# Softmax denominators of a second attention folded by accumulating DMAs within SBUF, and three smaller edits

## The chip, the cores and the metric

The kernel runs on one core of a Trainium2 chip. The metric is device time in microseconds (us), the median of several executions. In the profile PE is the matrix engine (PEld its weight loads), DVE the vector engine, ACT the scalar engine, POOL the GpSimd engine and SP the engine that here only issues DMAs. SBUF is the on-chip memory, of 128 partitions, and PSUM the memory that PE writes its results into.

## The reference, cut to what matters

The input `x` is 16 images of 256 channels by 1024 pixels, float32. Each image goes through a first attention over its pixels (4 heads of 64 channels), with a residual, and then through a second block: group norm, attention (8 heads of 32 channels), residual, group norm, a two-layer MLP with gelu, residual.

```python
x = _L0_conv_ref(x, w_proj, b_proj, w_out, b_out)      # attention, 4 heads of 64, + x
x = x + attention(group_norm(x, gn1_w, gn1_b), qkv_w, proj_w, proj_b, phys_bias)
h = group_norm(x, gn2_w, gn2_b)
h = einsum('oc,bchw->bohw', mlp_w1, h) + mlp_b1        # 256 -> 1024
h = gelu(h)
h = einsum('oc,bchw->bohw', mlp_w2, h) + mlp_b2        # 1024 -> 256
return x + h
# in attention(): softmax over m of (q k * scale + phys_bias), then times v
```

The change concerns the softmax of the second attention. Its denominator, the sum of exp(score) over the 1024 keys, is one number for each head and query.

## The kernel before, in words

**Tiling.** Channels lie on partitions, in CC = 2 chunks of 128. Queries go in NT = 2 blocks `t` of TB = 512, keys in SB = 8 blocks `kb` of 128. A score tile has 128 keys on its partitions and 512 queries along them, so the sum over the keys is a sum over partitions and over key blocks.

**One item of the second attention (`attention_b`, L508).** An item is a pair (t, c): 512 queries and the G = 4 heads of one channel chunk. There are four items per image, in the order (1,0), (0,0), (0,1), (1,1) (L513). Each item is cut into four units of two key blocks, so an image has 16 units. For each unit:

- `scores` (L518) makes s_b on PE (L532) and e_b = exp(s_b) on ACT (L547).
- `add` (L553) sums the e_b of all key blocks on DVE into es_b (L563). An item's es_b is two tiles of 128 x 1024, that is 128 x 512 for each of its four heads; tag "es" has four buffers.
- `weigh` (L579) multiplies e_b by v on PE (acc_b, L584) and adds it up in res_b (L597).

**Denominators.** A step after an item's last `weigh`, `normalise` (L601) sums es_b over the partitions: four matmuls on PE (L606), one for each head, with 32 columns of (scaled) ones, `eones`, as weights and 512 columns of es_b passing through. The result den_b in PSUM is 128 x 512: 32 equal rows for each head. `denominators` (L357) then copies it on ACT into rd_b (L358; tag "full", one buffer for all items), takes one row of 32 by a DMA of SP's queue to 128 x 16 (sp_b, L363), takes the reciprocal on DVE (L367), writes it by a DMA to DRAM (row_b, L368), and reads it back, broadcast, by four DMAs into the same rd_b (L373). POOL adds up the denominators and their inverses for a check at the end (L369, L370). At last `scale` (L629) multiplies res_b by rd_b on DVE (L631). After the second chunk of a block t, `project` multiplies the block by the output weights on PE (the tiles j, L344).

**Steps.** `attention_a` and `attention_b` are generators; each `yield` ends a step. `run` (L1036) calls `later.tick()` after every step, which runs what was put off by `later.after(n, ...)`, and then the pieces of `fill` for that step: projections and MLP products of neighbouring images, for PE to do beside the second attention. With L625 the steps of an item's denominators are put off by (1, 1) and for an image's last item by (3, 5). The last item's `project` is `handed` (L635) to the next image's `attention_a`, which calls it at its unit n = SB + 4 (L486).

**Order of the instructions.** A planner in the build rearranges the emitted instructions on each engine by modelled times, within the dependences; instructions in `keep_in_program_order` keep theirs. So the order on an engine is near the emitted one and not the same.

**Between two images.** After `attention_b` of image b comes `attention_0` of image b + 1, in which the last item's denominators are finished beside the first units of `attention_a`. On SP's queue there lie in the same stretch the load of the MLP weights for image b (`load_blocks(1, ...)`, L1103, L278; 1.8 MB from DRAM), an output store (L1023, 256 KB) and the load of a later image's x (`load_x`, L1100, L322; 1 MB).

**Other places that the change touches.** `attention_a` (L384) has es_a tiles (L430) of the same tag "es". `v` in the projections of q, k and v copies PSUM to SBUF on ACT (L800). `mlp` has a hidden stage with gelu on ACT (L919, L931), after which the next exp of `attention_b` needs another table of ACT (15 `ACT_TABLE_LOAD` at L547). Of POOL's DMAs before, the profile has those at the start (L152 to L161), which load and store weights.

Of the kernel before, what the change touches and what calls it, by code (L numbers as in the profile page):

```python
# [11 lines left out]
ALU = mybir.AluOpType  # L12
# [42 lines left out]
def kernel(  # L55
# [144 lines left out]

    ebias = const.tile([P, HEADS1], F32, name="ebias")
    eones = const.tile([P, HEADS1, D1], F32, name="eones")

    def exp_bias():
        nc.scalar.activation(ebias, pb, AF.Exp)
        nc.vector.tensor_copy(eones, ebias.unsqueeze(2).to_broadcast([P, HEADS1, D1]))


    def scale_v():
# [9 lines left out]
    with ExitStack() as first:  # L219
        first_pass(  # L220
            first, tc, x, out,
            dict(
                wp=wp, bqk=bqk, pb=pb, bo=bo, g1w=g1w, g1b=g1b, g2w=g2w,
                g2b=g2b, pjb=pjb, m1b=m1b, m2b=m2b, wo=wo, wq=wq, wpj=wpj,
                m2b2=m2b2, gavg=gavg, mhalf=mhalf, ones=ones, eones=eones,
                bvo=bvo, at_start=at_start, load_rest=load_rest, exp_bias=exp_bias,
                scale_v=scale_v,
                make_blocks=make_blocks,
                in_range=in_range,
            ),  # L230
        )
# [15 lines left out]
def first_pass(ctx, tc, x, out, k):  # L247
# [106 lines left out]

    def denominators(key, den, d, full, waits, then):  # L357
        nc.scalar.copy(d, den)  # L358
        n = full.shape[1]
        w = 4 * TB // P  # L360
        spread = work.tile([P, w], F32, tag="spread", name=f"sp_{key}", bufs=2)
        row = dram.tile([4 * TB // n, n], F32, tag="row", name=f"row_{key}", bufs=4)
        nc.sync.dma_start(spread, d[::32].rearrange("p (a b) -> p a b", b=w))  # L363

        def invert():
            inverse = work.tile([P, w], F32, tag="inverse", name=f"inv_{key}", bufs=2)
            tc.keep_in_program_order(nc.vector.reciprocal(inverse, spread))  # L367
            nc.sync.dma_start(row.rearrange("r (a b) -> (r a) b", b=w), inverse)  # L368
            nc.gpsimd.tensor_add(dsum, dsum, spread)  # L369
            nc.gpsimd.tensor_add(isum, isum, inverse)  # L370
            num = P * n // (4 * TB)
            for r in range(P // num):
                nc.sync.dma_start(  # L373
                    full[r * num : (r + 1) * num], row[r].partition_broadcast(num)
                )
            later.after(waits[1], lambda: then(full))

        later.after(waits[0], invert)
# [5 lines left out]
    def attention_a(b, qT, kT, v, project):  # L384
# [4 lines left out]
        accs, held, sums = {}, {}, {}  # L389

        def scores(i, kb):
            t, c = items[i]
# [16 lines left out]
        def weigh(i, kb, e):  # L409
            t, c = items[i]  # L410
            if kb == 0:
                if i % 2:
                    acc = wide(f"acc_{key}_{i}", 2)
                    accs[i] = [acc[:, h, :] for h in range(2)]
                else:
                    accs[i] = [bank(f"acc_{key}_{i}_{h}", h) for h in range(2)]
            for h in range(2):
                for g in range(2):
                    nc.tensor.matmul(  # L419
                        accs[i][h][g * D : (g + 1) * D, :],  # L420
                        v[h * HALF : (h + 1) * HALF, kb, c * 2 + g],
                        e[h * HALF : (h + 1) * HALF, g, :],
                        start=(kb == 0),
                        stop=(kb == SB - 1),
                    )
            if kb == 0:
                held[i] = e
                return
            if kb == 1:
                sums[i] = work.tile([P, 2, TB], F32, tag="es", name=f"es_{key}_{i}", bufs=4)  # L430
            nc.vector.tensor_add(sums[i], held[i] if kb == 1 else sums[i], e)  # L431
            if kb == SB - 1:
                r = res[:, c, t * TB : (t + 1) * TB]
                one, two = accs.pop(i)
                nc.scalar.copy(r, one)
                nc.vector.tensor_add(r, r, two)
                if i == len(items) - 1:
# [70 lines left out]
    def attention_b(b, qT, kT, v, project):  # L508
# [1 line left out]
        G = P // D  # L510


        items = [(NT - 1, 0)]  # L513
        items += [(t, 0) for t in range(NT - 1)] + [(t, 1) for t in range(NT)]
        units = [(i, kb) for i in range(len(items)) for kb in range(0, SB, 2)]
        res, sums = {}, {}

# [34 lines left out]

        def add(i, kb, es, which):  # L553
            if kb == 0 and 0 in which:
                sums[i] = [
                    work.tile([P, 2, TB], F32, tag="es", name=f"es_{key}_{i}_{n}", bufs=4)
                    for n in range(G // 2)
                ]
            for n in which:
                if kb == 0 and n < G // 2:  # L560
                    continue
                d = sums[i][n % 2]
                ins = nc.vector.tensor_add(d, es[n % 2] if kb == 0 else d, es[n])  # L563
                if n:
                    tc.keep_in_program_order(ins)
# [1 line left out]


        def result(t):
            if t < NT - 1 and b == 0:  # L570
                return [
                    work.tile([P, TB], F32, tag="g", name=f"res_{key}_{t}_{c}", bufs=16)
                    for c in range(CC)
                ]
            tag = "res1" if t == NT - 1 else "res" if b < B - 1 else "q0"
            r = act.tile([P, CC, S if tag == "q0" else TB], F32, tag=tag, name=f"res_{key}_{t}")
            return [r[:, c, :TB] for c in range(CC)]

        def weigh(i, kb, es):  # L579
            t, c = items[i]  # L580
            acc = bank(f"acc_{key}_{i}_{kb}", 0)
            for m in range(2):
                for g in range(G):
                    nc.tensor.matmul(  # L584
                        acc[g * D : (g + 1) * D, :],
                        v[:, kb + m, c * G + g],
                        es[2 * m + g // 2][:, g % 2, :],
                        start=(m == 0),
                        stop=(m == 1),
                    )  # L590
            if t not in res:
                res[t] = result(t)
            r = res[t][c]
            if kb == 0:
                nc.scalar.copy(r, acc)
            else:
                nc.vector.tensor_add(r, r, acc)  # L597
            if kb == SB - 2:
                later.after(1, lambda: normalise(i, r, i == len(items) - 1))

        def normalise(i, r, last):  # L601
            t, c = items[i]
# [2 lines left out]
            for g in range(G):  # L605
                nc.tensor.matmul(  # L606
                    den[g * D : (g + 1) * D, :],
                    k["eones"][:, c * G + g],
                    sums[i][g // 2][:, g % 2, :],
                    start=True,  # L610
                    stop=True,
                )
            full = work.tile([P, TB], F32, tag="full", name=f"rd_{key}_{i}", bufs=1)
            if at_end:
# [6 lines left out]
                    nc.gpsimd.tensor_add(tot[:, :1], tot[:, :1], part)  # L621
                return
            denominators(
                f"{key}_{i}", den, full, full,
                (3, 5) if last else (1, 1),  # L625
                lambda full: scale(i, r, last, full),
            )

        def scale(i, r, last, full):  # L629
# [139 lines left out]
    def qkv(key, D, src, weights, b_qk, qT, kT, v_dst):  # L769
# [16 lines left out]
                )  # L786

        def v(n):
            ps = single(f"v_{key}_{n}")
# [10 lines left out]
            nc.scalar.copy(  # L800
                v_dst()[:, 2 * n : 2 * n + 2],
                ps.rearrange("p (b h d) -> p b h d", b=2, d=D),
            )
# [91 lines left out]
    def mlp(b, xb):  # L895
# [44 lines left out]
            gelu(0, 1, i, ps[:, 1, :])  # L940

        def finish(i):
            ps = open_sums.pop(i)
            products_of(i, [(7, ps[:, 0, :], False), (6, ps[:, 1, :], False)])
            rest = gs[1, 1, i]
# [3 lines left out]
            gelu(1, 1, i, rest)  # L949
            combine((1, 0), (0, 0), False, i)  # L950
            combine((0, 1), (1, 1), False, i)

        hidden = [
            lambda part=part, i=i: part(i)
# [138 lines left out]

    later.after(2, fold_bias)
    later.after(8, k["scale_v"])
    hidden, outputs = [], []
    last = NT * CC * SB // 2 - 1
    for b in range(B):
# [41 lines left out]
            now, end = outputs[:3], outputs[3:]  # L1140
        if not first:

            fill = {m: [piece] for m, piece in enumerate(own[:5:2] + own[1::2] + own[6:])}
            fill.update({len(own) + 3 * m: [piece] for m, piece in enumerate(now)})
            now = []

# [331 lines left out]
```

## Time and profile before

| | us |
|---|---|
| median of 3 runs | 3666.4 (3665.53 to 3667.68) |
| the profiled execution | 3666.7 |
| its span in the trace | 3664.9 |
| TensorE clock granted, mean | 0.999 |
| one image, from its unit to the same unit of the next | 226.4 |

The span is the time between the first and the last instruction; 1.8 us of the execution lie around it. The period of one image is the distance of the same instruction in two successive images late in the run (3228.21 and 3454.65). The core spends nearly the whole span in 16 such periods, and 15 passages from the second attention of one image to the first attention of the next.

The groups of most weight besides the ones shown in the prediction, in the page's form (line, engine, operation, out<-in, shapes, count, busy us, mean ns, idle before and who ended it):

```profile
L563 DVE TENSOR_TENSOR es_b<-es_b,e_b 128x1024 f32<-128x1024 f32 x768 | 899.3, 1219 | 243.8 <-ACT e_b L547 243.8
L547 ACT ACTIVATE e_b<-s_b 128x1024 f32<-128x1024 f32 (+1 forms) x1280 | 982.9, 864 | 132.2 <-PE s_b L532 132.0
L406 ACT ACTIVATE e_a<-s_a 128x1024 f32<-128x1024 f32 x512 | 521.2, 1025 | 360.0 <-PE s_a L398 347.6
L532 PE MATMUL s_b<-q,k 32*64 32x512 f32 x8192 | 519.7, 600 | 4.9 <-DVE res_b L597 1.6
L584 PE MATMUL acc_b<-e_b,v 128*32 128x512 f32 x4096 | 492.1, 598 | 0.0
```

PE's matmuls overlap: [...]the busy time divided by the count (519.7 / 8192 = 63 ns) is nearer to what one costs[...].

### The profile page before, as it was taken

How to read it: one execution, taken by the hardware profiler on the slowest of the kernel's cores; microseconds unless marked ns; L12 is line 12 of the kernel's file. 1: busy time of each engine (PE TensorE's matmuls, PEld its weight loads, DVE VectorE, ACT ScalarE, POOL GpSimd, SP SyncE). 2: the span in 40 equal slices, each digit the busy share in tenths (PEclk: the TensorE clock that was granted, in tenths of full speed). 3: DMA queues.
4: the chain of work that ended last, by engine and by line, in shares of the span. 5: the costliest groups of instructions: out<-in, count | busy, mean ns of one | idle time of the engine just before them, and what ended most of it. 6: DMA issues, size and time to landing. Idle time of an engine off the chain costs nothing.

```text
span 3664.9 us, 79373 instructions
## 1 busy us (share of the span) xinstructions
PE 3632.6 (99%) x34221; PEld 1346.2 (37%) x34221; DVE 2658.1 (73%) x3424; ACT 2154.3 (59%) x2832; POOL 129.5 (4%) x266
## 2 busy tenths in 40 slices
PE   9999999999999999999999999999999999999999
PEld 3433343333433334333343333434334343343433
DVE  4586777767777677776767777677777777767777
ACT  4665657556565655656556565564655656556572
POOL 3000000000000000000000000000000000000000
PEclk9999999999999999999999999999999999999999
DMA  4000110101101011010110101101011010100100
GB/s 147 10 17 29 55 33 14 51 30 54 33 14 51 30 54 33 14 51 31 53 33 20 51 27 51 33 19 50 27 51 33 19 50 29 50 33 31 47 28 27
DMA packets 66549, 138.36 MB, mean 38 GB/s; under 512 B 35630, under 2 KB 36398, under 8 KB 61966
## 3 DMA queue, kind: packets, MB, share of 16 engines
q1 hardware_dynamic: 63116, 126.64, 10.7%
q8 instruction: 270, 4.42, 0.5%
q0 software_dynamic: 1328, 6.17, 0.5%
q14 instruction: 89, 0.73, 0.1%
q10 hardware_dynamic: 1746, 0.40, 0.1%
HBM read 111.17 MB, written 21.23 MB: 36 GB/s over the span
## 4 chain that ended last, share of the span: by engine, by line
PE 91%; DVE 4%; ACT 3%; DMA 1%; issue 1%; SPq 0%; ACTq 0%; POOL 0%; DVEq 0%
PE s_a L398 12%; PE acc_b L584 12%; PE s_b L532 12%; PE acc_a L419 12%; PE m L344 10%; PE m L906 9%; PE qk_a L344 6%; PE qk_b L344 5%; PE v_a L344 3%; PE j L344 3%; PE v_b L344 2%; ACT e_b L547 2%; PE o L344 2%; PE den_b L606 1%; DVE g L962 1%
## 5 line engine op out<-in xcount | busy, mean ns | idle before, releaser
L563 DVE TENSOR_TENSOR es_b<-es_b,e_b 128x1024 f32<-128x1024 f32 x768 | 899.3, 1219 | 243.8 <-ACT e_b L547 243.8
L547 ACT ACTIVATE e_b<-s_b 128x1024 f32<-128x1024 f32 (+1 forms) x1280 | 982.9, 864 | 132.2 <-PE s_b L532 132.0
L406 ACT ACTIVATE e_a<-s_a 128x1024 f32<-128x1024 f32 x512 | 521.2, 1025 | 360.0 <-PE s_a L398 347.6
L398 PE MATMUL s_a<-q,k 64*64 64x512 f32 x4096 | 544.3, 593 | 0.0
L419 PE MATMUL acc_a<-e_a,v 64*64 64x512 f32 x4096 | 540.1, 589 | 0.0
L532 PE MATMUL s_b<-q,k 32*64 32x512 f32 x8192 | 519.7, 600 | 4.9 <-DVE res_b L597 1.6
L431 DVE TENSOR_TENSOR es_a<-es_a,e_a 128x1024 f32<-128x1024 f32 x384 | 473.9, 1234 | 64.8 <-ACT e_a L406 41.2
L584 PE MATMUL acc_b<-e_b,v 128*32 128x512 f32 x4096 | 492.1, 598 | 0.0
L344 PE MATMUL m<-g,w 128*32 128x512 f32 (+1 forms) x3320 | 404.3, 592 | 0.0
L532 PEld LDWEIGHTS s_b<-q,k 32*64 32x64 f32 x8192 | 170.9, 130 | 321.3 <-issue 130.9
L419 PEld LDWEIGHTS acc_a<-e_a,v 64*64 64x64 f32 x4096 | 187.9, 133 | 251.5 <-issue 218.4
L398 PEld LDWEIGHTS s_a<-q,k 64*64 64x64 f32 x4096 | 175.9, 133 | 246.7 <-issue 193.1
L563 DVE TENSOR_TENSOR es_b<-e_b,e_b 128x1024 f32<-128x1024 f32 x128 | 150.8, 1220 | 153.4 <-ACT e_b L547 153.4
L906 PE MATMUL m<-gn_h,w 128*128 128x512 f32 x512 | 243.7, 604 | 5.7 <-DVE g L932 3.3
L584 PEld LDWEIGHTS acc_b<-e_b,v 128*32 128x32 f32 x4096 | 108.5, 109 | 357.5 <-ACT e_b L547 194.7
L344 PE MATMUL qk_a<-x,wp 128*32 128x512 f32 (+1 forms) x1856 | 235.1, 593 | 4.1 <-ACT k L784 4.1
L344 PE MATMUL qk_b<-gn_g,wq 128*32 128x512 f32 (+1 forms) x1280 | 234.0, 592 | 0.0
L597 DVE TENSOR_TENSOR res_b<-res_b,acc_b 128x512 f32<-128x512 f32 x192 | 131.8, 686 | 129.8 <-PE acc_b L584 129.8
L344 PEld LDWEIGHTS m<-g,w 128*32 128x32 f32 (+1 forms) x3320 | 121.4, 112 | 262.3 <-issue 235.3
L962 DVE TENSOR_TENSOR g<-g,g 128x512 f32<-128x512 f32 x320 | 206.3, 681 | 4.0 <-ACT g L919 2.8
L906 PE MATMUL m<-hs,w 128*128 128x512 f32 x384 | 177.9, 592 | 0.1
L919 ACT ACTIVATE g<-g,m1b 128x512 f32<-128x512 f32 x128 | 92.2, 722 | 99.3 <-DVE g L946 72.2
(147 smaller groups left out, 2803.6 us busy)
## 6 DMA issues: line engine op xcount, KB each, us to landing
w<-w_kept SPq DMA_DIRECT2D x30, 1792.0 KB
d_a<-row_a SPq DMA_DIRECT2D x64, 256.0 KB
rd_b<-row_b SPq DMA_DIRECT2D x252, 64.0 KB
out_dram<-x SPq DMA_DIRECT2D x63, 256.0 KB
x<-in_x_dram SPq DMA_DIRECT2D x30, 512.0 KB
w_kept<-w_made POOLq DMA_DIRECT2D x2, 1792.0 KB, 6.0
w_made<-in_L_conv_mlp_w_dram POOLq DMA_DIRECT2D x8, 256.0 KB, 6.1
x<-in_x_dram SPq DMA_DIRECT2D x4, 256.0 KB
```

What stands on the lines that cost most here:

```text
L344: nc.tensor.matmul(o[sl], w[:, sl], r, **flags)
L398: nc.tensor.matmul(s[h : h + HALF, g, :], kT[g * D : (g + 1) * D, c, kb * P + h : kb * P + h + HALF], qT[g * D : (g + 1) * D, c, t * TB : ...
L406: nc.scalar.activation(e, s, AF.Exp, scale=float(D) ** -0.5)
L419: nc.tensor.matmul(accs[i][h][g * D : (g + 1) * D, :], v[h * HALF : (h + 1) * HALF, kb, c * 2 + g], e[h * HALF : (h + 1) * HALF, g, :], st ...
L431: nc.vector.tensor_add(sums[i], held[i] if kb == 1 else sums[i], e)
L532: nc.tensor.matmul(outs[g][h : h + HALF, :], kT[g * D : (g + 1) * D, c, k0 : k0 + HALF], qT[g * D : (g + 1) * D, c, t * TB : (t + 1) * TB] ...
L547: nc.scalar.activation(to, s, AF.Exp, scale=float(D) ** -0.5)
L563: ins = nc.vector.tensor_add(d, es[n % 2] if kb == 0 else d, es[n])
L584: nc.tensor.matmul(acc[g * D : (g + 1) * D, :], v[:, kb + m, c * G + g], es[2 * m + g // 2][:, g % 2, :], start=(m == 0), stop=(m == 1),)
L597: nc.vector.tensor_add(r, r, acc)
L906: nc.tensor.matmul(ps, blocks[1][number - 1][:, i * P : (i + 1) * P], inputs[b][number], start=first, stop=True, skip_group_check=not first,)
L962: (nc.vector.tensor_add if plus else nc.vector.tensor_sub)(d, d, gs[(*what, i)])
```

## The change

Four edits, cut to their core (line numbers in the diff are those of before, then after).

1. The items of every image go in the order of t: (0,0), (0,1), (1,0), (1,1). Which tags hold res_b changes with it, and so do the pieces of `fill` in the first and the last image.
2. For the first three items of an image, `fold` takes the place of the matmuls over es_b. es_b has four groups of 32 partitions, each holding, for all four heads, the sums over a quarter of the key positions (32 x 4 x 512 numbers, 256 KB). A DMA of SP's queue copies the first group, repacked, into a tile `packed` of 128 x 512, and the three other groups are added to it by three DMAs of POOL's queue with `accum_op=ALU.add`. Three steps later `normalise_folded` sums what is left with four matmuls of 128 columns each, with other weights (`folded`, made once at the start by a memset and eight small DMAs on POOL). den_b is then 128 x 128, and the ACT copy, the row and its broadcast (pieces of 512 bytes) have that shape. The fourth item keeps the old way, with (3, 5); the folded ones have (1, 1).
3. es_b of an item becomes one tile of 128 x 4 x 512 with two buffers, and es_a of two items one tile of the same tag.
4. Two ticks after the last `finish` of the hidden stage, `back_to_exp` runs an Exp on one column, and the first copy of v in the second attention's projection goes to DVE.

```diff
+    def fold_ones():
+        nc.gpsimd.memset(folded, 0.0)
+        g_num = P // D1
+        w = D1 // g_num
+        for c in range(HEADS1 // g_num):
+            for g in range(g_num):
+                nc.gpsimd.dma_start(
+                    folded[g::g_num, c, g * w : (g + 1) * w],
+                    eones[g::g_num, c * g_num + g, :w],
+                )
...
-        nc.sync.dma_start(spread, d[::32].rearrange("p (a b) -> p a b", b=w))
+        nc.sync.dma_start(
+            spread, d[:: 32 // parts].rearrange("p (a b) -> p a b", b=w)
+        )
...
-                sums[i] = work.tile([P, 2, TB], F32, tag="es", name=f"es_{key}_{i}", bufs=4)
+                if c == 0:
+                    both[t] = work.tile([P, 2 * CC, TB], F32, tag="es", name=f"es_{key}_{t}", bufs=2)
+                sums[i] = both[t][:, 2 * c : 2 * c + 2]
...
-        items = [(NT - 1, 0)]
-        items += [(t, 0) for t in range(NT - 1)] + [(t, 1) for t in range(NT)]
+        items = [(t, c) for t in range(NT) for c in range(CC)]
...
-                later.after(1, lambda: normalise(i, r, i == len(items) - 1))
+                if i == len(items) - 1:
+                    later.after(1, lambda: normalise(i, r, True))
+                else:
+                    fold(i, r)
+
+        def fold(i, r):
+            packed = work.tile([P, TB], F32, tag="packed", name=f"packed_{key}_{i}", bufs=1)
+            for j in range(G):
+                of = sums[i][j * D : (j + 1) * D]
+                if j == 0:
+                    nc.sync.dma_start(packed, of)
+                else:
+                    nc.gpsimd.dma_start(packed, of, accum_op=ALU.add)
+            later.after(3, lambda: normalise_folded(i, r, packed))
+
+        def normalise_folded(i, r, packed):
+            c = items[i][1]
+            q = TB // G
+            den = bank(f"den_{key}_{i}", 1)[:, :q]
+            for n in range(G):
+                nc.tensor.matmul(
+                    den[n * D : (n + 1) * D, :], k["folded"][:, c],
+                    packed[:, n * q : (n + 1) * q], start=True, stop=True,
+                )
+            full = work.tile([P, TB], F32, tag="full", name=f"rd_{key}_{i}", bufs=1)
+            denominators(
+                f"{key}_{i}", den, full[:, :q], full, (1, 1),
+                lambda full: scale(i, r, False, full), G,
+            )
...
         def finish(i):
+            if i == n4 - 1:
+                later.after(2, back_to_exp)
...
+        def back_to_exp():
+            one = small.tile([P, 1], F32, tag="part", name=f"one_{b}")
+            nc.scalar.activation(one, gs[1, 1, n4 - 1][:, :1], AF.Exp, scale=0.0)
...
+    later.after(9, k["fold_ones"])
...
-            fill = {m: [piece] for m, piece in enumerate(own[:5:2] + own[1::2] + own[6:])}
+            fill = {0: own[:1], 1: own[1:3], 2: own[4:5], 3: own[5:6], 4: own[3:4], 5: own[6:]}
```

More of the change, by code (lines that the diff above doesn't have):

```diff
@@ L202 @@
     eones = const.tile([P, HEADS1, D1], F32, name="eones")
+    folded = const.tile([P, HEADS1 * D1 // P, D1], F32, name="folded")
     def exp_bias():
@@ L226 @@
                 bvo=bvo, at_start=at_start, load_rest=load_rest, exp_bias=exp_bias,
-                scale_v=scale_v,
+                scale_v=scale_v, fold_ones=fold_ones, folded=folded,
                 make_blocks=make_blocks,
@@ L344, in product, with denominators @@
             nc.tensor.matmul(o[sl], w[:, sl], r, **flags)
-    def denominators(key, den, d, full, waits, then):
+    def denominators(key, den, d, full, waits, then, parts=1):
         nc.scalar.copy(d, den)
@@ L372, in invert @@
             for r in range(P // num):
-                nc.sync.dma_start(
-                    full[r * num : (r + 1) * num], row[r].partition_broadcast(num)
-                )
+                to, of = full[r * num : (r + 1) * num], row[r]
+                if parts > 1:
+                    to = to.rearrange("p (n q) -> p n q", n=parts)
+                    of = row.rearrange("r (a q) -> (r a) q", a=parts).rearrange(
+                        "(n g) q -> g n q", n=parts
+                    )[r]
+                nc.sync.dma_start(to, of.partition_broadcast(num))
             later.after(waits[1], lambda: then(full))
@@ L388, in attention_a @@
         res = act.tile([P, CC, S], F32, tag="res", name=f"res_{key}")
-        accs, held, sums = {}, {}, {}
+        accs, held, sums, both = {}, {}, {}, {}
         def scores(i, kb):
@@ L554, in add @@
             if kb == 0 and 0 in which:
[L555 to L558, printed above, removed]
+                sums[i] = work.tile([P, G, TB], F32, tag="es", name=f"es_{key}_{i}", bufs=2)
             for n in which:
@@ L561, in add @@
                     continue
-                d = sums[i][n % 2]
+                d = sums[i][:, n % 2 * 2 : n % 2 * 2 + 2]
                 ins = nc.vector.tensor_add(d, es[n % 2] if kb == 0 else d, es[n])
@@ L569, in result @@
         def result(t):
[L570 to L577, printed above, removed]
+            tag, n = ("hs", 3) if t == NT - 1 else ("res1", CC)
+            r = act.tile([P, n, TB], F32, tag=tag, name=f"res_{key}_{t}")
+            return [r[:, c] for c in range(CC)]
         def weigh(i, kb, es):
@@ L608, in normalise @@
                     k["eones"][:, c * G + g],
-                    sums[i][g // 2][:, g % 2, :],
+                    sums[i][:, g, :],
                     start=True,
@@ L623, in normalise @@
             denominators(
-                f"{key}_{i}", den, full, full,
-                (3, 5) if last else (1, 1),
-                lambda full: scale(i, r, last, full),
+                f"{key}_{i}", den, full, full, (3, 5), lambda full: scale(i, r, last, full)
             )
@@ L788, in v @@
         def v(n):
+            copy = nc.vector.tensor_copy if not n and b_qk is None else nc.scalar.copy
             ps = single(f"v_{key}_{n}")
@@ L799, in v @@
                     )
-            nc.scalar.copy(
+            copy(
                 v_dst()[:, 2 * n : 2 * n + 2],
```

## The prediction

> **What bounds the kernel now.** I read the page's busy times and the chain that ended last first, then the groups and waits of the operations that the change touches, then the timeline of one passage between two images.
>
> ```profile
> PE 3632.6 (99%) x34221; PEld 1346.2 (37%) x34221; DVE 2658.1 (73%) x3424; ACT 2154.3 (59%) x2832; POOL 129.5 (4%) x266
> PE 91%; DVE 4%; ACT 3%; DMA 1%; issue 1%; SPq 0%; ACTq 0%; POOL 0%; DVEq 0%
> ...
> L606 PE MATMUL den_b<-es_b,eones 128*32 128x512 f32 x512 | 67.4, 592 | 0.0
> L547 ACT ACT_TABLE_LOAD x15 | 19.2, 1283 | 0.3
> ...
> PE v_b L344 <- ACT e_b L547: 10.2, 15, 0.7
> ```
>
> PE sets the time: what is taken from PE is won, and where PE stands still it is lost. The denominators of the second attention are 67.4 us of busy time, and there is one wait of 0.7 us for an exp in each image but one. This is all there is to win. POOL is nearly empty.
>
> In the timeline (start, length, engine and line) the price of one item's denominator matmuls is the distance of neighbours:
>
> ```profile
> 1484.55 1.04 PE L584 MATMUL acc_b<-e_b,v 128*32 128x512 f32 x8
> 1485.41 1.04 PE L606 MATMUL den_b<-es_b,eones 128*32 128x512 f32 x8
> 1486.27 3.62 PE L344 MATMUL m<-g,w 128*32 128x512 f32 x32
> ```
>
> 0.86 us from den_b to the next work, for eight records (two for each float32 matmul), that is two rounds of 0.43 us over four column strips.
>
> The passage after an image's last item, where T = 1563.52 is the start of s_b of its last unit:
>
> ```profile
> 1563.52 1.97 PE L532 MATMUL s_b<-q,k 32*64 32x512 f32 x32
> 1567.16 3.62 PE L344 MATMUL j<-res_b,wpj 128*32 128x512 f32 x32
> 1570.60 3.62 PE L344 MATMUL m<-g,w 128*32 128x512 f32 x32
> 1568.02 3.49 DVE L563 TENSOR_TENSOR es_b<-es_b,e_b 128x1024 f32<-128x1024 f32 x3
> 1574.27 0.34 SPq L278 DMA_DIRECT2D w<-w_kept  x1
> 1577.47 1.04 PE L606 MATMUL den_b<-es_b,eones 128*32 128x512 f32 x8
> 1578.44 2.81 PE L398 MATMUL s_a<-q,k 64*64 64x512 f32 x24
> 1578.58 0.59 ACT L358 COPY rd_b<-den_b 128x512 f32<-128x512 f32 x1 [0.27 <-PE den_b L606]
> 1579.66 2.85 ACT L406 ACTIVATE e_a<-s_a 128x1024 f32<-128x1024 f32 x3 [0.49 <-PE s_a L398]
> 1583.66 0.38 SPq L368 DMA_DIRECT2D row_b<-inv_b  x1
> 1589.09 1.72 SPq L373 DMA_DIRECT2D rd_b<-row_b  x4
> 1592.72 0.69 DVE L631 TENSOR_TENSOR res_b<-res_b,rd_b 128x512 f32<-128x512 f32 x1 [3.98 <-DMA rd_b<-row_b]
> ```
>
> The reader is to see that PE goes from one group to the next, that ACT copies den_b at once into a free rd_b, and that transfers are slow here: the row, issued behind 1 MB of loads of x, lands after 5.4 us (1583.66 to 1589.09).
>
> [...]the trace of the start has 0.7 to issue and 2.2 to land (below), 2.9. [...]no trace here shows an accumulating DMA. [...]
>
> **The change part by part.**
>
> *Folded denominators, 48 of 64 items.* Four matmuls of 128 columns take the place of four of 512. Streaming falls from 0.43 to 0.107 us a round, and a round's weight loads (0.13 us for four at this shape) then set it: 2 x 0.13 = 0.26. Won: 0.60 each (0.55 to 0.64), x 48 = 28.6 us.
>
> *Their transfers.* One item: a copy by SP, then three accumulating DMAs on POOL, each waiting for the one before, as all write the same tile. The nearest rows:
>
> ```profile
> 32.93 3.02 POOL L152 DMA_DIRECT2D w_made<-in_L_conv_mlp_w_dram  x4 [6.00 <-DMA w_kept<-w_made]
> 38.19 2.07 POOL L160 TENSOR_TENSOR w_made<-w_made 128x512 f32<-128x512 f32 x1 [2.23 <-DMA w_made<-in_L_conv_mlp_w_dram]
> ```
>
> Issue 0.75 plus 2.23 is 3.0 us, and 0.8 for the second read (256 KB at the 323 GB/s that the queue moves when busy): 3.8. The first copy is 2.0 (the usual landing of sp_b) + 0.8 = 2.8. Chain: 2.8 + 3 x 3.8 = 14.1 us. It starts at the last add (T' + 8.0 in an item's last step, 1571.5) and PE wants it some two and a half steps of 7.2 us later, T' + 25: 17 us are there. So it is hidden up to 4.7 us for each accumulating DMA. [...] POOL's other work, the check sums, may be late at no cost.
>
> *Dummy Exp.* It moves the table load ahead of the first exp: 15 x 0.68 = 10.2 us won; at worst nothing.
>
> *Order of the items.* The number of matmuls is unchanged and so are the changes of tile shape. But the planner's order, read from the built program, is what counts. With t in order, item 2 is (1,0), and its denominators, due (1, 1), fall into the last step and the passage. The instructions of the passage, the same in 15 passages:
>
> ```
> SP   sp_b_2; w load (waits PE); row_b_2 (waits DVE); out store; rd_b_2 x4; x loads; sp_b_3
> DVE  adds of the last unit; reciprocal of item 2; x; res_b; es_a (2 adds); scale of item 2
> ACT  e_a 0 to 3; copy rd_b_3 <- den_b_3; e_a 4
> PE   den_b_3; s_a 0 to 2; acc_a half 0, kb 0; s_a 3; acc_a half 0, kb 1; s_a 4, one; acc_a half 1
> ```
>
> **A new wait.** rd_b has one buffer. The copy of item 3 must wait until item 2's scale has read it; before, that scale was done at T + 1.4, long ahead of the copy. Behind the waiting copy stand on ACT e_a 4 and all later exps; behind the copy on PE is acc_a half 1, since it takes the bank of den_b_3. Step by step: without j (3.44 us, now in another step) m ends at T + 7.1, so the w load is issued at T + 7.3 and s_a starts at S0 = T + 11.5 (14.9 less 3.44). The reciprocal is behind the adds (end T + 8.0), so the row is issued at T + 8.3, behind 1.8 MB. Load and store moved data until 6.9 us after the load's issue in this passage, so the row lands at T + 14.2. The broadcast ends 3.63 us after its first issue (1589.09 to 1592.72): T + 17.8. Scale 0.69, copy 0.6: acc_a half 1 starts at T + 19.3. From S0 that is 7.8 us, in which PE has 4.5 us of work: s_a 4 x 0.86, halves of acc_a 2 x 0.43, 0.2 of s_a 4. It loses 3.3, and 1.1 more since half 1 then runs alone on half of the array. 4.4 us a passage. From below: if the DMAs were free, scale still comes behind two es_a adds that need e_a 2 (S0 + 4.1): at the earliest scale ends at S0 + 6.0, which leaves 2.1 by standing still; with the adds one behind the other, 3.7 in all. From above 5.5, when x and store traffic delay the broadcast. 14 x 4.4 + 3.8 (the first, with a bare step) = 65.4. The last image has no passage, but its reciprocal goes into the same buffer: +3 (0 to 5).
>
> *Edits at nothing.* The eight small DMAs of `folded` lie at the start, and weights stored behind them are read 280 us later. The copies on ACT get shorter; ACT is at 59%. One copy of v to DVE: 0.6 us per image on an engine at 73%; DVE bounds bare steps alone (images 0 and 15). es_a and es_b have the same bytes and lifetimes. Scales of items 0 and 1 find their rows a step earlier than needed. Without this cover each is below 1 us an image.
>
> **Sum,** against the profiled execution, 3666.7: - 28.6 - 10.2 + 65.4 + 3.0 = 3696.3. The median is 0.3 below it, so 3696, 0.8% slower.
>
> **The rivals.**
>
> *A, as summed: the new wait costs more than the saving.* Per passage 3.4 to 5.5 us: 3677 to 3716. For it: the built order leaves no other way, and the only unmeasured part is how long. The saving is 38.8 us, so it decides from 38.8 / 15 = 2.6 us a passage.
>
> *B, the tile comes free early: faster.* Row and broadcast pass the weight load[...], and the half-filled array costs nothing because ACT had exps ready ahead. PE then stands still only from S0 + 4.5 to a copy at S0 + 6: 1.5 us. 3666.4 - 38.8 + 22.5 = 3650. Against it: the scale's place behind two adds on DVE.
>
> *C, accumulating DMAs late.* Above 4.7 us each, PE waits at the folded matmuls, three times the excess for some 45 items: at 5.2 another 67 us (3763), at 6.1 another 190 (3885). For it the landing of 6.1 on the page; against it the chain at the start, 3.0 for one.
>
> *D, they cancel.* 2.1 to 3.1 us a passage: within 7 us of 3666.
>
> **How the numbers follow.** A 0.57, B 0.20, C 0.13, D 0.10. 0.2%, 7.3 us, is about what a measurement of this kernel can tell. A and C are slower, 0.70; D the same, 0.10; B faster, 0.20. The predicted time is A's. The range takes in A, D and the nearer ends of B and C: 3648 to 3745, leaving out half of B and most of C; A's own is 3677 to 3716.
>
> **What would show it.** Right: den_b at half of its busy time or less, no table load between the gelu and v_b that PE waits for, and in each passage an idle time of PE and of ACT's copy of some 3 to 5 us, released by DVE's scale, which waits for rd_b. Wrong: the copy waits below 2 us (B or D), or PE waits for `packed` at the folded matmuls (C).

## The result, and the profile after

The changed kernel takes 3891.4 us (median of four, 3884.4 to 3896.0) against 3666.4 before: a ratio of 1.061, with a 95% interval from 1.059 to 1.063. It is slower by 225 us, where 30 were forecast.

The page of the changed kernel, its busy times and the chain that ended last:

```profile
PE 3720.7 (96%) x34221; PEld 1392.1 (36%) x34221; DVE 2670.0 (69%) x3440; ACT 2132.7 (55%) x2833; POOL 264.2 (7%) x419
PE 71%; DMA 19%; DVE 5%; issue 2%; SPq 1%; ACT 1%; ACTq 0%; DVEq 0%; POOLq 0%
```

DMA was 1% of the chain and is 19% now. PE does the same number of matmuls, 48 items of them shorter, and is busy 88 us longer: so the matmuls themselves ran slower. The mean granted clock is 0.978 instead of 0.999, and 2.1% of the span is 82 us. The waits of PE (engine, who waited for whom, us in total, times, longest):

```profile
PE den_b L631 <- DMA packed_b<-es_b: 81.1, 31, 6.7
PE acc_a L438 <- ACT rd_b L371: 46.6, 15, 4.6
```

The first is rival C, the second is forecast A. Both happened.

**The chain of accumulating DMAs.** The timeline of the first item of one image (start, length, engine and line; in brackets the idle time ahead and who ended it):

```profile
1572.23 0.60 SPq L621 DMA_DIRECT2D packed_b<-es_b  x1
1576.38 0.91 POOL L623 DMA_DIRECT2D packed_b<-es_b  x1 [44.38 <-PE m L357]
1581.33 0.90 POOL L623 DMA_DIRECT2D packed_b<-es_b  x1 [4.03 <-DMA packed_b<-es_b]
1586.43 0.88 POOL L623 DMA_DIRECT2D packed_b<-es_b  x1 [4.21 <-DMA packed_b<-es_b]
1591.34 0.42 PE L631 MATMUL den_b<-packed_b,folded 128*32 128x128 f32 x8 [1.73 <-DMA packed_b<-es_b]
```

From one accumulating DMA to the next are 5.1 us in the median: 0.9 to issue, 4.2 until the next can follow. The copy ahead takes 4.2 us. The chain takes 19.1 us here and 19 to 21 in every image. Of the 48 folded items 32 make PE wait: the first and second of every image, 1.6 to 3.5 us each in the middle images and up to 9 in the first and the last.

**The passage between two images.** Seven images in, the weight load, the row of the third item, its broadcast, scale, the copy and acc_a:

```profile
1670.38 0.35 SPq L291 DMA_DIRECT2D w<-w_kept  x1
1671.23 0.32 SPq L383 DMA_DIRECT2D row_b<-inv_b  x1
1678.68 1.74 SPq L394 DMA_DIRECT2D rd_b<-row_b  x4
1682.33 0.69 DVE L669 TENSOR_TENSOR res_b<-res_b,rd_b 128x512 f32<-128x512 f32 x1 [2.10 <-DMA rd_b<-row_b]
1683.10 0.59 ACT L371 COPY rd_b<-den_b 128x512 f32<-128x512 f32 x1 [2.94 <-DVE res_b L669]
1683.74 0.84 PE L438 MATMUL acc_a<-e_a,v 64*64 64x512 f32 x2 [2.97 <-ACT rd_b L371]
```

This is the forecast's chain, link by link: the row lands 7.4 us after its issue behind the load, the broadcast ends 3.65 us after its first issue, and PE stands still for 3.0 us. DVE had ended its two adds into es_a at 1680.23 and stood 2.1 us for the broadcast, so in the end the transfers set the time.

**The clock.** PE in two stretches of 3.41 us around that wait (stretch, us, busy, matmuls, granted clock, DMA share, GB/s):

```profile
1680.65:1684.06 3.41, 0.44 (x4) 1.00 0.85 235
1684.06:1687.47 3.41, 3.41 (x18) 0.50 0.35 120
```

After the wait the clock falls to half for 3.4 us, which costs 1.7 us more. This is what the busy time hides, and the forecast had left it out.

**Where the time is, by stage.** I call "passage" the distance from an image's first s_a to its first s_b, and "second attention" that from its first s_b to the next image's first s_a, both read from the trace. Passages before are 101.8 us long, after 110.1 in the median. The second attention of a middle image was 124.6 and is 128.3, that of the first image 90.2 and 112.6. Summed over the span: passages +124 us, second attention of the middle images +51, of the first image +22, and what follows the last image's first s_b +29. The two kinds of stage are the two axes of all experiments.

### The profile page after: what moved, and what is told of

It reads as the page before. It is cut to its first block, busy times and chain, and to the rows that moved or that the text cites. A ratio compares the mean times of both kernels' runs of the same rounds, so it can differ in the third digit from the quotient of the medians.

```text
span 3893.6 us, 79815 instructions
## 1 busy us (share of the span) xinstructions
PE 3720.7 (96%) x34221; PEld 1392.1 (36%) x34221; DVE 2670.0 (69%) x3440; ACT 2132.7 (55%) x2833; POOL 264.2 (7%) x419
## 4 chain that ended last, share of the span: by engine, by line
PE 71%; DMA 19%; DVE 5%; issue 2%; SPq 1%; ACT 1%; ACTq 0%; DVEq 0%; POOLq 0%
DMA packed_b<-es_b 13%; PE acc_a L438 12%; PE s_a L417 10%; PE s_b L552 9%; PE acc_b L596 7%; PE m L357 7%; PE m L945 6%; PE qk_b L357 5%; PE qk_a L357 3%; DMA row_b<-inv_b 3%; PE j L357 3%; PE v_b L357 3%; PE v_a L357 2%; PE o L357 2%; DMA rd_b<-row_b 1%
## 5 line engine op out<-in xcount | busy, mean ns | idle before, releaser
L438 PE MATMUL acc_a<-e_a,v 64*64 64x512 f32 x4096 | 626.0, 609 | 46.6 <-ACT rd_b L371 46.6
L417 PE MATMUL s_a<-q,k 64*64 64x512 f32 x4096 | 637.6, 605 | 0.0
L552 PE MATMUL s_b<-q,k 32*64 32x512 f32 x8192 | 530.6, 606 | 4.4 <-ACT q L820 1.4
L438 PEld LDWEIGHTS acc_a<-e_a,v 64*64 64x64 f32 x4096 | 215.1, 137 | 330.6 <-issue 258.7
L417 PEld LDWEIGHTS s_a<-q,k 64*64 64x64 f32 x4096 | 200.5, 135 | 251.9 <-issue 234.4
L357 PE MATMUL qk_a<-x,wp 128*32 128x512 f32 (+1 forms) x1856 | 250.6, 627 | 5.6 <-ACT k L822 5.6
L623 POOL DMA_DIRECT2D packed_b<-es_b x144 | 128.8, 894 | 1233.7 <-PE m L357 621.7
```

The costliest lines, as they stand in the source:

```text
L357: nc.tensor.matmul(o[sl], w[:, sl], r, **flags)
L417: nc.tensor.matmul(s[h : h + HALF, g, :], kT[g * D : (g + 1) * D, c, kb * P + h : kb * P + h + HALF], qT[g * D : (g + 1) * D, c, t * TB : ...
L438: nc.tensor.matmul(accs[i][h][g * D : (g + 1) * D, :], v[h * HALF : (h + 1) * HALF, kb, c * 2 + g], e[h * HALF : (h + 1) * HALF, g, :], st ...
L552: nc.tensor.matmul(outs[g][h : h + HALF, :], kT[g * D : (g + 1) * D, c, k0 : k0 + HALF], qT[g * D : (g + 1) * D, c, t * TB : (t + 1) * TB] ...
```

## The experiments

In the table, medians over the images, without the first passage and with the first image's second attention apart. For each run's ratio the kernel before was timed beside it (3667 to 3668 us).

| run | us | ratio, 95% interval | passage | second attention | the same, first image |
|---|---|---|---|---|---|
| before | 3666.4 | | 101.8 | 124.6 | 90.2 |
| changed | 3891.4 | 1.059 to 1.063 | 110.1 | 128.3 | 112.6 |
| e1_tile_apart | 3762.9 | 1.025 to 1.028 | 101.8 | 127.8 | 111.7 |
| e2_step_later | 3844.7 | 1.047 to 1.051 | 109.6 | 126.0 | 105.4 |
| e3_both | 3733.9 | 1.016 to 1.020 | 101.8 | 126.8 | 105.7 |
| e5_no_fold | 3665.5 | 0.999 to 1.000 | 101.8 | 123.8 | 90.2 |
| e6_scale_later | 3718.4 | 1.011 to 1.015 | 101.8 | 126.8 | 106.8 |
| e7_middle_images | 3698.6 | 1.007 to 1.010 | 101.8 | 126.8 | 90.2 |
| e8_plain_copies | 3776.7 | 1.028 to 1.032 | 109.9 | 121.8 | 98.9 |
| e9_exp_alone | 3655.4 | 0.995 to 0.998 | 101.8 | 123.8 | 90.2 |
| e10_all_a_step_later | 3653.8 | 0.995 to 0.998 | 103.0 | 121.8 | 90.2 |
| e11_w_load_behind | 3796.9 | 1.034 to 1.037 | 102.8 | 128.4 | 112.9 |
| e12_half_transfers | 3779.1 | a single run | 110.4 | 121.8 | 100.7 |
| e13_loads_behind | 3626.4 | 0.987 to 0.991 | 101.8 | 121.8 | 90.2 |

### The wait at the passages

```diff
         def normalise(i, r, last):
...
-            full = work.tile([P, TB], F32, tag="full", name=f"rd_{key}_{i}", bufs=1)
+            full = work.tile([P, TB], F32, tag="packed", name=f"rd_{key}_{i}", bufs=1)
```

> The changed kernel, but the last item's rd_b takes the buffer of `packed` (free by then) instead of the one that the third item's scale still reads. Theory 1 (the wait at the passages between images is real, costs PE 3.0 us of standing still in each, 1.1 us of a half-filled array, and what a lower granted clock after it costs): 15 x (3.1 + 1.1) = 63 us, and about 15 x 2.5 = 40 us of the 85 us of lost clock go: about 3790 us, clock about 0.99, no wait of PE's acc_a for ACT's rd_b. Rival (the passage only waits because the folded items are late already, and the time is lost elsewhere): within 30 us of the changed kernel, 3860 or more.

3762.9 us, 128 less than the changed kernel; the wait of acc_a is gone and the passages are at 101.8 again. The one buffer that the last item's copy shared with the third item's scale is shown to cost over half of the loss. It was more than expected, about 8 us a passage; the expectation had 4.2 and some 2.5 of clock.

The same wait from its other end, the transfer that scale waits for:

```diff
         if b:
-            load_blocks(1, b - 1)
+            later.after(4, lambda b=b: load_behind(1, b - 1))
...
+    def load_behind(m, b):
+        with tc.issue_after(sent[0].ins):
+            load_blocks(m, b)
...
-                nc.sync.dma_start(to, of.partition_broadcast(num))
+                sent[:] = [nc.sync.dma_start(to, of.partition_broadcast(num))]
```

> The changed kernel, with the load of the MLP weights in the passage issued behind the last item's broadcast instead of ahead of the third item's row. Theory 1 (the row waits behind the 1.8 MB, as forecast): the row lands in 3 us instead of 7.3, scale is 3 to 4 us earlier and held only by the two es_a adds, PE stands still for 1 us or less in a passage instead of 3.0 and the clock stays up; from s_a to s_b 103 to 105 us instead of 110; about 3800 us. Theory 2 (the place of scale behind two adds on DVE sets it, as the bound from below said: 2.1 us of standing still): 107 us or more, about 3850.

3796.9 us, and 102.8 instead of 110.1 in the passages. Of PE's waits there this is left:

```profile
PE acc_a L444 <- ACT rd_b L377: 5.3, 6, 1.7
```

The number is theory 1's: with the row no longer behind 1.8 MB the wait is nearly gone (5.3 us in all, 46.6 in the changed kernel). But the run does not test theory 2. With the load moved, the order on DVE changed too, as the planner sets it: scale comes ahead of the two adds in 14 of the 15 passages, as here, where s_a starts at 1870.15:

```profile
1871.83 0.69 DVE L675 TENSOR_TENSOR res_b<-res_b,rd_b 128x512 f32<-128x512 f32 x1 [3.44 <-DMA rd_b<-row_b]
1873.28 1.23 DVE L458 TENSOR_TENSOR es_a<-e_a,e_a 128x1024 f32<-128x1024 f32 x1 [0.76 <-ACT e_a L431]
```

What scale's place behind the adds costs by itself stays open. In the changed kernel's passage above PE stood 3.0 us and DVE 2.1 for the broadcast; the difference, 0.9 us, is an estimate of it. The 1.0 us that most passages still lose here has no lost clock and no longer wait of PE than before the change; that it is one half of acc_a running alone (1.1 forecast) is not shown. In the changed kernel's passage above, that half alone (4 records at 1678.89) took 0.86 us to the next work, as both halves together (8 records at 1689.78) did.

### The chain

```diff
-            later.after(3, lambda: normalise_folded(i, r, packed))
+            later.after(3 if i == 2 else 4, lambda: normalise_folded(i, r, packed))
```

> The changed kernel, but the folded matmuls of the first and second item of an image are put off by one more step; the third keeps its place. Theory 1 (a chain of one copy and three accumulating DMAs takes 19.5 us, 5.1 us for each accumulating one, and PE waits at the folded matmuls of these two items, 90 us, with lost clock of about 45 us after it): these waits go, about 3755 us. What is left is then what was forecast, 3696, plus the clock that the waits at the passages cost, some 40. Rival (DMA queues are simply full, so that a later place waits too): waits of den_b for packed_b above 40 us are left.

3844.7 us, a gain of only 47. Where the matmuls were put off (the chain's end is now some 5 us ahead of them in the middle images) they don't wait: den_b's waits fall from 81 to 26 us, which are the first and last image and the third item. But new ones stand in the list, 36 us of s_b for DVE. e3 shows them without the passages.

> Both edits together. Theory 1 (two waits of PE and the clock that they cost explain the whole loss; the saving of 28.6 us on the matmuls and of 10.2 us on the exp is real): 3625 to 3645 us, clock 0.998 or above, faster than before the change by about 1%. Rival (the traffic of the accumulating DMAs, or the order of the items, costs time of its own): between 3666 and 3720.

3733.9 us, outside both expectations, if nearer to the rival. The edits together leave 126.8 us in each second attention; 121.8 will prove possible (e8). The list of waits has:

```profile
PE s_b L552 <- DVE x L1062: 20.2, 14, 2.2
PE s_b L552 <- DVE res_b L609: 18.6, 16, 4.2
```

and the timeline of one of them:

```profile
2269.52 2.40 SPq L394 DMA_DIRECT2D rd_b<-row_b  x4
2275.38 0.69 DVE L669 TENSOR_TENSOR res_b<-res_b,rd_b 128x512 f32<-128x512 f32 x1 [1.91 <-DMA rd_b<-row_b]
2275.99 0.74 DVE L1062 SCALAR_TENSOR_TENSOR x<-m,m2b,x 128x512 f32<-128x512 f32 x1
2276.79 1.09 PE L552 MATMUL s_b<-q,k 32*64 32x512 f32 x8 [1.05 <-DVE x L1062]
```

A broadcast beside the next item's accumulating DMAs takes 5.9 us here. The third item's, of the same form and with none of them beside it, takes 3.3 to 3.7 in most images, and in e8, with plain copies beside it, the first two items' take about 4.9. DVE stands at scale, behind scale stands the add that frees a PSUM tile, and PE's s_b wants that tile. So I put scale off by a step:

```diff
-                f"{key}_{i}", den, full[:, :q], full, (1, 1),
+                f"{key}_{i}", den, full[:, :q], full, (1, 2),
```

> The kernel with both edits (3734 us), and besides the scale of a folded item is put off by one more step. Theory (a third wait: the row of a folded item and its broadcast now take 3.0 and 5.9 us beside the accumulating transfers, DVE stands at the scale, and what is behind it on DVE, the add that frees the PSUM tile of m or acc_b, makes PE's s_b wait: 39 us of waits in 30 places, with some 15 us of lost clock): these waits of s_b go, about 3680 us, and the stretch from the first s_b to the next s_a falls from 126 to 127 us to about 122 to 123 us. Rival (the transfers are late whatever the place, so the wait moves with the scale): within 15 us of 3734.

3718.4 us, 15.5 less, at the rival's edge (within 15) and not by its mechanism: the waits of s_b went, but the second attention stayed at 126.8, because the third item, no longer delayed by the first two, now waited itself: 48 us of den_b for packed_b in 18 places, about 2.1 us in each middle image. The expectation was wrong by not looking at who is late next.

The first and the last image without folding:

```diff
+                elif b in (0, B - 1):
+                    later.after(1, lambda: normalise(i, r, False))
                 else:
                     fold(i, r)
```

> As the run before it, and besides the first and the last image are not folded at all (their steps are 5 us long and three of them are shorter than the chain of 19.5 us). Theory: the waits of den_b for packed_b that are left, 21 us in 6 places, and the clock lost after them go, against 6 x 0.6 us of saving given up: 25 to 35 us less than the run before it, about 3645 to 3655, faster than the kernel before the change. Rival (the accumulating traffic costs time everywhere): no faster than 3667.

3698.6 us, 20 less: the first image is at 90.2 again. The theory's difference was nearly right (25 to 35 expected), its total not. The total is the rival's (no faster than 3667), and its cause is not: the third item still waits, and the next run takes that away with the same traffic.

And the third item's matmuls put off too:

```diff
-            later.after(3 if i == 2 else 4, lambda: normalise_folded(i, r, packed))
+            later.after(4, lambda: normalise_folded(i, r, packed))
```

> As the run with the middle images folded (3699 us), and the folded matmuls of the third item are put off by a step too, like the first two. Theory (what is left there is the wait of den_b for packed_b of the third item, 2.1 us in each middle image, with 1.7 us of lost clock after most of them and the rest beside it; nothing else stands in the way of the saving): the stretch from the first s_b to the next s_a falls from 126.8 to about 122 us, as in the run with plain copies, 14 x 4.8 = 67 us: about 3632 us, faster than every kernel so far. Rival (its row and broadcast come a step later, behind the weight load, and the wait returns at the scale or at the product that the next image does): 3655 or more.

3653.8 us, 45 less; the second attention is 121.8 in every image, as the theory says, with no wait for packed_b. The total is just under the rival's (3655 or more), and the rest of the expected 67 came back as the rival said: the third item's broadcast lies with the loads of weights and x, DVE stands about 5 us at its scale (up to 5.8), and the next image's group norm makes PE wait 15.9 us in 13 places.

### What an accumulating DMA costs

```diff
-                    nc.gpsimd.dma_start(packed, of, accum_op=ALU.add)
+                    nc.gpsimd.dma_start(packed, of)
```

> The changed kernel, with three plain copies in the place of the three accumulating ones, on the same queue, in the same chain and of the same size (so the sums of three of four key groups are left out). Theory 1 (the addition makes the transfer longer, as forecast with 0.8 us for the second read): a link of the chain falls from 5.1 to about 3.8 us and the chain from 19.5 to about 15.5, so most of the waits at den_b go, and the time falls by 90 to 130 us. Theory 2 (the price lies in issue and landing of a DMA that POOL issues, within SBUF, and the addition is nearly free): links of 4.8 to 5.1 us, and a time within 20 us of the changed kernel.

and, with the adding kept and 128 KB instead of 256:

```diff
-                    nc.gpsimd.dma_start(packed, of, accum_op=ALU.add)
+                    nc.gpsimd.dma_start(packed[:, : TB // 2], of[:, :, : TB // 2], accum_op=ALU.add)
```

> The changed kernel, with the three accumulating DMAs carrying half of the columns (128 KB instead of 256 KB each; the sums of the other half of three key groups are left out). Theory 1 (an accumulating DMA is a fixed price and a price per byte[...]): a link falls from 5.1 to about 3.7 us. Theory 2 (the price is fixed): above 4.7 us.

Two links of e8 and one of e12 in the timelines:

```profile
604.39 0.54 POOL L623 DMA_DIRECT2D packed_b<-es_b  x1 [3.06 <-DMA packed_b<-es_b]
608.03 0.54 POOL L623 DMA_DIRECT2D packed_b<-es_b  x1 [3.11 <-DMA packed_b<-es_b]
```

```profile
607.76 0.90 POOL L623 DMA_DIRECT2D packed_b<-es_b  x1 [2.78 <-DMA packed_b<-es_b]
```

In the median a plain copy of 256 KB is a link of 3.8 us (0.54 to issue), an accumulating one 5.1 (0.89), an accumulating one of half the size 3.7 (0.89). So the addition costs 1.4 us in a link of 256 KB, 0.35 of it in the issue, and the second 128 KB of an accumulating DMA cost 1.4 us, by estimate about 92 GB/s. Both links are as theory 1 of each run had them. e8 took 3776.7 us, 115 less, and e12 about as much. In both runs den_b of the first two items comes 17.2 us after the first copy's issue, with next to no wait in the middle images, and the second attention is 121.8: with links below 4.3 us ((17.2 - 4.2) / 3) there is nothing to wait for.

### The small edits

Folding taken out, the rest left:

```diff
                 else:
-                    fold(i, r)
+                    later.after(1, lambda: normalise(i, r, False))
...
-                f"{key}_{i}", den, full, full, (3, 5), lambda full: scale(i, r, last, full)
+                f"{key}_{i}", den, full, full, (3, 5) if last else (1, 1),
+                lambda full: scale(i, r, last, full)
```

> The changed kernel without folding: all four items take the old matmuls over es_b, one step after their last weigh; order of the items, tiles and dummy Exp as in the changed kernel. Theory 1 (only folding and its lateness hurt): 3666 less 10 us for the dummy Exp, about 3656; the third item's scale comes two steps earlier, so the passage does not wait. Rival (the order of the items brings the wait at the passages by itself): 3690 or more, with PE's acc_a waiting for ACT's rd_b.

and the dummy Exp and the copy of v alone, in the kernel before (the lines of the change, nothing else):

```diff
+            copy = nc.vector.tensor_copy if not n and b_qk is None else nc.scalar.copy
...
         def finish(i):
+            if i == n4 - 1:
+                later.after(2, back_to_exp)
```

> The kernel before the change, with the dummy Exp and the copy of v on DVE alone. Theory (the 10.2 us of waits of v_b are won, as forecast; without folding, the changed kernel won only 2 us since its order of work in the first and the last image costs 10): about 3655 us, 0.3% faster. Rival (the wait is worth nothing, PE waits for the next exp instead): 3664 or more.

e9 gains 12 us, 0.9 in each second attention, near the forecast (10.2); its two edits are not told apart. e5 gains the same 0.9, and yet comes out with no change that can be told: its second image's passage takes 108.1 instead of 101.8 us, and 4 to 5 go in the last image. The order of the items and the pieces of work in these two images, where steps are bare, costs about 10 us, as e13 confirms by giving them back. The passages of e5 don't wait, so the order alone does not bring the passage's wait; with folding, which puts the third item two steps later, it does.

### Everything together

e13 is e10 with the loads of weights and of x behind the last broadcast, and with the order of items, the tiles of the results and the fill of before in the first and last image.

```diff
         items = [(t, c) for t in range(NT) for c in range(CC)]
+        if b in (0, B - 1):
+            items = [(NT - 1, 0)]
+            items += [(t, 0) for t in range(NT - 1)] + [(t, 1) for t in range(NT)]
...
-            fill = {0: own[:1], 1: own[1:3], 2: own[4:5], 3: own[5:6], 4: own[3:4], 5: own[6:]}
+            fill = {m: [piece] for m, piece in enumerate(own[:5:2] + own[1::2] + own[6:])}
...
+        def issue_behind():
+            with tc.issue_after(sent[0].ins):
+                issue()
...
+        if b < 2:
+            issue()
+        else:
+            later.after(4, issue_behind)
```

> As the run with all folded items a step later (3654 us), and besides two edits. The loads of the MLP weights and of x in the passage are issued behind the last item's broadcast; and the first and the last image have the item order and the pieces of work between steps of the kernel before the change. Theory (DVE stands 5 us at the third item's scale, since its broadcast shares the queue with 2.8 MB, and that makes the group norm of the next image late, 1.2 us from s_a to s_b in each passage; and the order of work in the first image costs 6.3 us, seen as 108.1 instead of 101.8 in its passage, with some 4 in the last): from s_a to s_b 101.8 everywhere, 14 x 1.2 + 6 + 4 = 27 us less, about 3628 us, 1.1% faster than before the change. Rival (the weights and x are then late themselves, and PE waits for them in the next stage): 3645 or more.

3626.4 us: 1.1% faster than the kernel before, ratio 0.987 to 0.991, and all stages of the table at the lowest value that any run showed. Its busy times and the folded matmuls' group:

```profile
PE 3604.5 (99%) x34221; PEld 1343.2 (37%) x34221; DVE 2673.6 (74%) x3440; ACT 2132.6 (59%) x2833; POOL 298.7 (8%) x401
L660 PE MATMUL den_b<-packed_b,folded 128*32 128x128 f32 x336 | 16.9, 273 | 0.0
```

PE is at 99% again and has no idle time ahead of the folded matmuls. The gain of 41 us compares with a forecast saving of 38.8; 42 items are folded instead of 48.

## Why the prediction was wrong

**The direction was right, and so was the wait that was forecast; two prices were too small.** In the passages 65 us were forecast and 124 measured. Everywhere else 36 were to be won, and 102 were lost (51 + 22 + 29).

**The step that failed outside the passages is the price of the chain of transfers.** "Issue 0.75 plus 2.23 is 3.0 us, and 0.8 for the second read ... 3.8": a link measured 5.1. "The first copy is 2.0 ... + 0.8 = 2.8": it measured 4.2. So "14.1 us" was 19 to 21, where "17 us are there" was right (17.2), and rival C, given 0.13, came true along with A, not instead of it. With the copy at 4.2 the limit for a link was 4.3, not 4.7. e8 and e12 say which part of a link was mis-sized: a plain copy within SBUF is already 3.8 by POOL, not 3.0, and the addition costs 1.4, not 0.8. The 0.8 was an estimate, 256 KB at the 323 GB/s of queue q1 while busy (126.64 MB in 10.7% of 3664.9 us, by the page of the kernel before); that an addition costs such a second read was shown by no trace. The nearest row was a load from DRAM seen once at the start; the transfer of the change reads SBUF and repacks 32 partitions into 128. Which of these differences makes it longer is not shown. Taking away the additions alone won 115 us (3891.4 to 3776.7).

**The step that failed in the passages is the clock, which was put at nothing.** e8 shows that the link's price was not all: with nearly no wait for the chain left in the middle images it still took 81 us more than the 3696 forecast, 55 of them in the passages (121 for 65). The wait itself was right in its place and nearly in its length: standing still was 3.0 us (3.3 forecast). But a passage lost 8.3 (110.1 less 101.8), not 4.4. In the mean over the passages after the first, 2.7 of it is lost clock, 1.7 or 3.4 in each. A further 1.5 to 2.6 us is neither standing still nor clock; the half-filled array was forecast at 1.1 of it, and the rest is not explained. The bound "from below: if the DMAs were free" stays untested, since e11 moved scale as well.

The forecast priced every wait at its own length. In the passages of the changed kernel the 14 waits of 2.4 to 4.6 us at acc_a went with 1.7 or 3.4 us of lost clock each, the one of 1.1 us with none. Over its span the lost clock came to 85 us (the sum of what ten-microsecond stretches were granted below full), against 1.7 in the kernel before: 38 in the passages, 17 in the second attentions of the middle images, the rest in the first and the last image. Rival C had left it out too: at a link of 5.2 it said 3763.

**Rows a step earlier than needed: wrong.** The "edits at nothing" held that the scales of the first two items find their rows early. DVE waits 156 us at scale in the changed kernel (48 before), and in e3 that reaches PE for 39 us. The forecast took the landing of a broadcast from a quiet queue (3.63 us), and this change adds the traffic beside it (5.9).

**The gains were right.** The second attention falls by 0.9 us with the dummy Exp and the copy of v (0.68 forecast) and by another 1.9 for three folded items, 0.64 each (0.60 forecast). **The order of the items** was costed at nothing but for the new wait, and costs about 10 us in the two end images, as e5 and e13 bracket it.

## What to carry to other kernels

Price a chain of dependent DMAs by the same transfer in the same memory, and ask what the traffic does to transfers that were quick beside it (here 3.6 us became 5.9). A wait on the bounding engine can cost more than its length: here a wait of 3 us went with up to 3.4 us of lost clock, 6.4 in all. When one wait is removed, look for who is late next before the run: three times here the next one took its place, and only the run that settled all of them at once showed the whole saving. When one instruction is moved, read the new order on the other engines too: in e11 a second thing moved with it.

## What the runs showed of the hardware

- In the trace of the changed kernel the granted clock is 1.00 or 0.50, and between its first and its last change it stays at one value for 3.413 us or a multiple of that (the longest 75 times). So lost clock comes in steps of 1.71 us there.
- In the same trace, cut into stretches of 3.413 us at these changes, without the first 35 and the last 8 us, the clock of a stretch goes with how long PE stood still in the one before it (by the records of its matmuls). Of the full-speed stretches, all 24 with 2.1 us or more of standing still were followed by one at half speed, none of the 272 with less than 0.9, and 5 of the 32 between. The one at 1438.3 us, with 1.32 us of standing still, was followed by half speed; the one at 2066.4, with 2.01, was not; what decides there is not shown. Of the half-speed stretches, all 8 with 0.54 us or less of standing still were followed by a full one, and none of the 19 with 0.55 or more.
- An accumulating DMA within SBUF: 0.89 us to issue on POOL for both sizes, 4.8 us from issue to landing for 256 KB (the changed kernel) and 3.4 for 128 KB (e12), in the median; a plain one of 256 KB 0.54 and 3.4 (e8).
